# Between two steps of a graph kernel: other work put first, y pairs into period 0, and a list filled in long rows

## The chip, the cores and the metric

The kernel runs on one core of a Trainium2 chip. The metric is the device time of one execution in microseconds (us); the kernel before takes 1303.6 us, the median of three runs (1302.28 to 1304.17).

## The reference

N = 2708 nodes with D = 256 features and a sparse N x N matrix adj (about 0.3% of it, and the diagonal, is not zero). Everything is float32. Cut to what matters:

```python
x  = layernorm(x + relu(concat([x, adj @ x]) @ W0 + b0))          # layer 0
R  = adj + eye(N);  R = R / R.sum(-1)                             # layer 1
Xf = Xa = x;  Z = 0
for n in range(2):
    q, k  = Xa @ W1.T @ W2.T, Xa @ W3.T
    probs = softmax(q @ k.T)
    A     = probs, cut in each row to the largest that hold 0.9 of the mass, made to sum to 1
    Xf, Xa = R @ Xf, A @ Xa
    Z = Z + Xf @ U1[n].T + Xa @ U2[n].T
out = layernorm(x + layernorm(x + Z) * ln_g + ln_b)
```

So there are two attention steps (step 1 and step 2, n = 0 and 1), each with a threshold per row, and two products with R, which don't depend on the attention.

## The kernel before

**Tiling.** The rows are cut into NB = 22 blocks of 128 (the last, EDGE, has 20). Layer 0 runs over the blocks with dense products of adj and y0 = x @ W0's second half (L257; y0 itself is made at the start, L392, from xT, which SP's queue loads in seven pieces at L196). While it does, the columns of adj that are not empty are named, and lists of at most 128 x CC columns (CC = 7) are made for each block: list_d in DRAM is first filled with a default (L280 to L282: a constant in ix, sent out in pieces of seven numbers), and later the names are written over it, and ix is read back from it. With the lists, GpSimd (POOL) gathers rows by indirect DMA: of adj in step 1 (L367, kept in adjc_d), and of the vectors that R is multiplied with (L719).

**Step 1** goes block by block: logits (L507), exp, threshold on VectorE, then turn() transposes the kept probabilities (L527, copied by ScalarE at L530) and products() multiplies them (L564). step1_out returns three pieces of work, scale, turn_out and project (L687 to L703): they scale the result, transpose it into xaT_all, and make from it the query and key of step 2 and a part of Z. The pieces of block t run inside block t + 1; those of the last block, after its edge_sum (L236 to L245), run by themselves. ya_pair (L664 to L678) makes ya, the right side of step 2's products, for two blocks at a time: eight matmuls into one of two acc buffers in PSUM, and a copy by ScalarE. In the kernel before all eleven pairs are put between the steps: one inside edge_sum, one ahead of each piece of the last block, one after each of the logits of blocks 0 to 2, the others after that.

**Step 2** is a software pipeline of NB + 2 periods, each with NG = 6 slots (the loop at L1272 and in it over g). In period per, block per + 2 gets its logits and exps2, block per + 1 its tries of a level (try_act: four passes of ScalarE over a whole row, two in L966 and two in L969, whose output goes to a scratch tile scr that nobody reads), block per its level and candidates and block per - 1 its threshold, marks and mask on VectorE (vector_slots), and block per - 2 its transposes and products. Each engine takes its instructions in the order of this program. Block 0 doesn't get its tries from ScalarE but from VectorE (try_dve) and one pass of ScalarE (L966), all before period 0. The blocks' rows lie in a ring of five tiles: es[2], es[3], es[0], es[1] and a fifth, e4, which with scr shares the place of xaT_all (tag V).

**R's products** are cut into 2 x 22 x 8 = 352 units of two matmuls each (r_units, L749): seven pieces of gathered rows and one of the block's own. The table units says how many each period takes, spread over its slots; first = 16 are taken before period 0. The first unit of a block calls r_load for the next block: its seven gathers on POOL (y_load, two buffers yg, so that a buffer must have been read before), and its loads on SP. r_out scales a finished block on VectorE and SP stores it.

**The end of a block.** When a block has both its parts, a Final does the two layer norms, one period each. final_slot(i) sets their slots: in slot 3 the statistics of both new ones and those in their second norm (finals), in slot 5 the roots on ScalarE, in slot 0 of the next period the normalising on ScalarE and two tensor operations on POOL for each new one (L1207, L1208), which the second statistics (L1182) need.

Of the kernel before, what the change touches and what calls it, by code (L numbers as in the profile page):

```python
# [9 lines left out]
FP = mybir.dt.float32  # L10
I32 = mybir.dt.int32
# [9 lines left out]
P = 128  # L21
# [18 lines left out]
ML = 16  # L40
CW, CC = 128, 7
# [107 lines left out]
def fast_path(ctx, tc, c, flags, fint, xT_d, x_d, w0_d, b0_d, w1_d, w2_d, w3_d, u1_d, u2_d, g_d, b_d):  # L149
    nc = tc.nc  # L150
    N, D, DA, NB, DC, KH, CHS, rows = c.N, c.D, c.DA, c.NB, c.DC, c.KH, c.CHS, c.rows
    ident = c.ident
    adj_d, out_d, x1_d, za_d = c.adj_d, c.out_d, c.x1_d, c.za_d
    NW = SEG * NS
# [14 lines left out]
    def ps_acc(t=None):  # L169
        acc = ps.tile([P, CH], FP, tag="acc", name="acc")  # L170
        if t == NB - 1:
            nc.vector.memset(acc[:, :D + 1], 0.0)
        return acc

    def ps_misc():
        return ps.tile([P, CH], FP, tag="misc", name="misc")
# [56 lines left out]
    fold = small.tile([P, EW], FP, tag="fold", name="fold", bufs=1)  # L233
    nc.vector.tensor_reduce(fold, ident.rearrange("p (j i) -> p i j", i=EW), AX.X, ALU.add)

    def edge_sum(acc, n, stop=True, meanwhile=None):  # L236

        p = rows(EDGE)
        four = work.tile([P, 4, P], FP, tag="wT", name="four", bufs=3).rearrange("p k i -> p (k i)")
        nc.scalar.copy(four[:, :n], acc[:, :n])  # L240
        if meanwhile:
            meanwhile()
        whole = ps_misc() if meanwhile else ps_acc()
        nc.tensor.matmul(whole[:p, :n], lhsT=fold[:, :p], rhs=four[:, :n], start=True, stop=stop)
        return whole  # L245

# [18 lines left out]
    LAST = NB * P * NB - 1  # L265
# [11 lines left out]
    for y_d in (c.yf_d, c.v_d):  # L277
        nc.gpsimd.dma_start(out=y_d[rows(NB - 1):, NB - 1, :], in_=zero)
    ix = small.tile([P, NB, CC], I32, tag="ix", name="ix", bufs=1)
    nc.gpsimd.iota(ix.rearrange("p m c -> p (m c)"), pattern=[[0, NB * CC]], base=LAST, channel_multiplier=0)  # L280
    for i, (a, b) in enumerate(((0, ML), (ML, NB))):
        nc.gpsimd.dma_start(out=c.list_ds[i][:, :CW * CC].rearrange("m (p c) -> p m c", c=CC), in_=ix[:, a:b, :])  # L282
    before_m = small.tile([NB, 1], FP, tag="before_m", name="before_m", bufs=1)
    nc.gpsimd.iota(before_m, pattern=[[0, 1]], base=0, channel_multiplier=KS * CAP,
                   allow_small_or_imprecise_dtypes=True)
# [376 lines left out]
    def ya_pair():  # L662


        if not y_pairs:
            return
        t0 = y_pairs.pop(0)
        pz = ps_acc().rearrange("p (s d) -> p s d", d=D)
        for s in range(2):
            p, at = rows(t0 + s), (t0 + s) * P  # L670
            for j in range(DC):
                nc.tensor.matmul(pz[:p, s, :], lhsT=xaT_all[:, j, at:at + p], rhs=c.u2[:, j, 1, :],  # L672
                                 start=j == 0, stop=j == DC - 1)
        if rows(t0 + 1) == P:
            nc.scalar.copy(ya[:, t0:t0 + 2, :], pz)
            return
        for s in range(2):
            nc.scalar.copy(ya[:rows(t0 + s), t0 + s, :], pz[:rows(t0 + s), s, :])  # L678
# [218 lines left out]
    for t in range(NB):  # L897
        acc = ps_acc(t)
        part = exps1(t + 2) if t + 2 < NB else None
        b = None  # L900
        if t >= NB - 3:
            b = blocks[t - (NB - 3)] = Block(t - (NB - 3))
        ra_next = finish1(t + 1) if t + 1 < NB else None
        for g in range(NG):
            turn(t, g, x1, acc, es[t % 4])
            if ends and 1 <= g <= 3:
                ends[g - 1]()
            if g < NL and t + 3 < NB:
                logits1(t + 3, g)
            if b and g in (0, 2):  # L910
                lg = logits(1, b.t, g // 2)
                if g == 0:
                    shift(b, lg[0])
            if b and g in (1, 3):
                exps2(b, g // 2, *lg)
            if part and g in (3, 4):
                part(g - 3)
            products(1)
            if stores and stores[0][0] <= NG * t + g:
                adj_store(*stores.pop(0)[1:])  # L920
            if g == 2:
                if t + 3 < NB:
                    extract1(t + 3)
                if t < 9:
                    lists.take(2 * t + 2, 2 * t + 4)
                if t == 8:
                    lists.end()
            if (t, g) in at:
                adj_gather(at[t, g])
                stores += [(NG * t + g + i, at[t, g], i - 4) for i in (4, 5)]  # L930
            if (t, g) in y_at:
                name_y()
                y_load(0, y_at[t, g])
            if (t, g) == (NB - 1, 2):
                a_load(0)
        if t == EDGE:
            products(0)
            acc = edge_sum(acc, D, meanwhile=ya_pair)
        ends = step1_out(t, acc, ra)
        ra = ra_next  # L940
    assert not stores and not staged and not to_turn
    r_load(0, 0)
    for f in ends:
        ya_pair()
        f()
    ya_pair()
    for t in range(3):
        exps2(blocks[t], 2, *logits(1, t, 2))
        ya_pair()
    while y_pairs:  # L950
        ya_pair()

    tile1 = big.tile([P, 2 * NW], FP, tag="x1", name="w")
    low = tile1[:, :NW]
    w = tile1[:, NW:]
    tile2 = big.tile([P, 2 * NW], FP, tag="V", name="e4")
    nc.gpsimd.memset(tile2[:, N:NW], 0.0)
    ring.append(tile2[:, :NW])
    scr = tile2[:, NW:]

    def try_act(b, k, part):

# [261 lines left out]
    def final_slot(i):  # L1224


        if i == 2:
            while ready and len(new) < 2:
                new.append(Final(*ready.pop(0)))
                new[-1].load()  # L1230
        if i == 1:
            while done:
                done.pop().store()
        n = len(new) + len(finals)
        if i == 3:
            for k, f in enumerate(new + finals):
                f.stats(k)
        if i == 5 and n:
            roots(0, n)
        if i == 0 and n:  # L1240
            over(0, n)
            for f in finals:
                f.end()
            for f in new:
                f.middle()
            done[:] = finals
            finals[:] = new
            new.clear()
# [3 lines left out]

    each = NB * (CC + 1)
    first = 2 * (CC + 1)
    units = {0: CC + 1, 1: CC + 1}
    rest = each - first - sum(units.values())
    units.update({p: rest * (p - 1) // 8 - rest * (p - 2) // 8 for p in range(2, 10)})
    units.update({p: each * (p - 10) // 11 - each * (p - 11) // 11 for p in range(11, 22)})
    assert first + sum(units.values()) == 2 * each


    b0, b1, b2 = (blocks[t] for t in range(3))
# [7 lines left out]
    try_act(b0, 1, 0)  # L1270
    next_level(b0, 1)
    for per in range(NB + 2):  # L1272
        if per == NB + 1:
            tail.append(True)
        n_r = units.get(per, 0)
        b_act = blocks.get(per + 1)
        t_mul = per - 2 if per > 1 else None
        if t_mul is not None:
            accs[t_mul] = ps_acc(t_mul)
        b_exp = None  # L1280
        if per and per + 2 < NB:
            b_exp = blocks[per + 2] = Block(per + 2)
        vector = vector_slots(blocks.get(per), blocks.get(per - 1), begin_search(b_exp) if b_exp else None)
        for g in range(NG):
            n = n_r * (g + 1) // NG - n_r * g // NG
            now = later.pop(0)
            later.append([])
            if g == 0:
                if b_exp:
                    shift(b_exp, lg[0])  # L1290
                r_units(n)
            if t_mul == EDGE:
                if g == 0:
                    products(0)
                    products(0)
                    edge_product(ya, accs[EDGE], e2(EDGE))
            elif t_mul is not None:
                turn(t_mul, g, ya, accs[t_mul], e2(t_mul))
            if b_exp and g == 3:
                lg = logits(1, b_exp.t, 2)  # L1300
            if g == NG - 1 and 3 < per + 3 < NB:
                lg = logits(1, per + 3, 0)
            if g:
                r_units(n)
            if b_exp and g == 1:
                lg = logits(1, b_exp.t, 1)
            if t_mul is not None and t_mul != EDGE:
                products(2)
            if b_exp and g in (0, 1, 3):
                exps2(b_exp, (g + 1) // 2, *lg)  # L1310
            if b_act:
                for k, part in {0: ((0, 0),), 1: ((0, 1), (0, 2), (0, 3)), 2: ((1, 0),), 3: ((1, 1), (1, 2), (1, 3))}.get(g, ()):
                    try_act(b_act, k, part)
            next(vector)
            if g == 0:
                final_slot(0)
                if t_mul:
                    t = t_mul - 1
                    base = za_load(t)
                    later[1].append(lambda t=t, base=base: arrive(t, base, accs.pop(t), ras.pop(t)[:rows(t)]))  # L1320
            for f in now:
                f()
            if g and (per < NB + 1 or g < NG - 1):
                final_slot(g)
# [407 lines left out]
```

## Time and profile before

| | |
|---|---|
| median of 3 runs | 1303.6 us |
| the profiled execution | 1308.28 us |
| its span, first to last instruction | 1306.5 us |
| TensorE busy | 1236.7 us (95%) |
| VectorE busy | 997.3 us (76%) |
| ScalarE busy | 735.6 us (56%) |
| POOL busy | 641.9 us (49%) |
| mean granted TensorE clock | 0.980 |

In the profile PE is TensorE (PEld its weight loads), DVE is VectorE, ACT is ScalarE, POOL is GpSimd and SP the engine that issues most DMAs; "SPq" and the like are the issue of a DMA. A line of a timeline gives the start, the duration, engine, line of the code, operation and tiles, and in square brackets the idle time ahead of it and what ended it. "x8" at the end of a line says that eight instructions are merged in it. Times of the profile count from the span's start. Layer 0 lasts to about 288 us, step 1 to about 730, step 2 from there to the end.

### The profile page before, as it was taken

Reading aid. Unit: us, or ns where it says so; the run is one execution under the profiler, and the core shown is the slowest. Engines: PE = TensorE matmul, PEld = TensorE weight load, DVE = VectorE, ACT = ScalarE, POOL = GpSimd, SP = SyncE. Lnnn points to the kernel's source line nnn. Section 1 sums busy time; section 2 is a strip of 40 time slices with the busy share of each in tenths; the row PEclk is TensorE's granted clock in tenths of the full one; section 3 lists DMA queues with packets and bytes.
Section 4 is the critical chain, followed back from the end, with each engine's and each line's share of the span. In section 5 each row is a group of like instructions: output and inputs, shape, how many; then the busy total and the mean of one; then the engine's idle time right before and its main releaser. Section 6 shows DMA issues by size and latency. Waiting matters only on the chain.

```text
span 1306.5 us, 18895 instructions
## 1 busy us (share of the span) xinstructions
PE 1236.7 (95%) x5764; PEld 892.9 (68%) x5764; DVE 997.3 (76%) x3406; ACT 735.6 (56%) x1337; POOL 641.9 (49%) x594
## 2 busy tenths in 40 slices
PE   7999999979899999999999978999999999999975
PEld 5878778843477777777777556777765777766753
DVE  2455445884999997977771279989888999999996
ACT  1010110125456656655665488887888989989821
POOL 1000000002465442577666068878775778888850
PEclk9999999999999999999999888999999999999898
DMA  7455445423322220132324145565663645555551
GB/s 189 152 171 165 149 160 169 148 89 105 119 81 84 70 71 12 40 93 92 91 85 107 49 150 156 177 184 169 185 145 114 197 143 161 175 169 156 151 121 38
DMA packets 101704, 166.00 MB, mean 127 GB/s; under 512 B 17362, under 2 KB 74070, under 8 KB 101594
## 3 DMA queue, kind: packets, MB, share of 16 engines
q1 hardware_dynamic: 75308, 108.65, 26.0%
q0 software_dynamic: 20544, 51.17, 15.1%
q10 hardware_dynamic: 5742, 4.89, 1.4%
q8 instruction: 48, 0.79, 0.3%
q14 instruction: 62, 0.51, 0.1%
HBM read 130.74 MB, written 33.90 MB: 126 GB/s over the span
## 4 chain that ended last, share of the span: by engine, by line
PE 77%; DVE 10%; ACT 6%; DMA 3%; POOL 2%; issue 1%; SPq 0%; ACTq 0%; POOLq 0%; DVEq 0%
PE acc L564 26%; PE acc L257 16%; PE lg L507 9%; PE misc L749 9%; PE tr L527 7%; PE acc L651 2%; DVE e L1088 2%; DVE w L1083 2%; PE acc L462 2%; PE misc L426 2%; PE acc L672 2%; PE misc L699 2%; DMA xT<-in_xT 1%; POOL yg L719 1%; ACT e L844 1%
## 5 line engine op out<-in xcount | busy, mean ns | idle before, releaser
L530 ACT COPY wT<-tr 128x512 f32<-128x512 f32 (+2 forms) x258 | 132.0, 519 | 216.8 <-PE tr L527 215.8
L564 PE MATMUL acc<-x,wT 128*128 128x256 f32 (+1 forms) x924 | 230.5, 388 | 0.0
L564 PE MATMUL acc<-ya,wT 128*128 128x256 f32 (+1 forms) x924 | 228.1, 386 | 0.0
L719 POOL DMA_INDIRECT yg<-v_d,ix x154 | 196.6, 1277 | 59.8 <-issue 23.2
L719 POOL DMA_INDIRECT yg<-yf_d,ix x154 | 191.6, 1244 | 48.3 <-issue 23.1
L564 PEld LDWEIGHTS acc<-x,wT 128*128 128x128 f32 (+1 forms) x924 | 165.2, 189 | 71.0 <-issue 37.4
L257 PE MATMUL acc<-y,adj_t 128*128 128x257 f32 (+1 forms) x924 | 208.4, 381 | 0.0
L564 PEld LDWEIGHTS acc<-ya,wT 128*128 128x128 f32 (+1 forms) x924 | 170.6, 191 | 44.5 <-issue 24.0
L749 PE MATMUL misc<-yg,adj_t 128*128 128x256 f32 (+1 forms) x704 | 185.1, 396 | 14.0 <-DMA yg<-v_d,ix 6.6
L257 PEld LDWEIGHTS acc<-y,adj_t 128*128 128x128 f32 (+1 forms) x924 | 171.8, 189 | 32.7 <-issue 8.9
L367 POOL DMA_INDIRECT adj_t<-in_adj,ix x154 | 167.8, 1089 | 51.8 <-issue 44.1
L749 PEld LDWEIGHTS misc<-yg,adj_t 128*128 128x128 f32 (+1 forms) x704 | 124.2, 191 | 67.2 <-issue 21.5
L507 PE MATMUL lg<-k,q 64*128 64x512 f32 (+3 forms) x528 | 150.2, 596 | 14.0 <-ACT e L848 7.0
L527 PE MATMUL tr<-ident,e 128*128 128x128 f32 (+2 forms) x946 | 148.5, 276 | 7.5 <-DVE e L1088 6.3
L527 PEld LDWEIGHTS tr<-ident,e 128*128 128x128 f32 (+2 forms) x946 | 113.0, 140 | 52.1 <-issue 24.0
L334 POOL DMA_DIRECT2D part_d<-e x1 | 0.6, 573 | 290.3 <-DVE e L333 290.3
L966 ACT ACTIVATE e<-e,st 128x2708 f32<-128x2708 f32 (+1 forms) x43 | 113.5, 2640 | 0.1
L439 ACT COPY x1T<-tr 128x256 f32<-128x256 f32 (+1 forms) x22 | 8.0, 364 | 186.6 <-PE tr L438 186.6
L969 ACT ACTIVATE e<-e,st 128x2708 f32<-128x2708 f32 (+1 forms) x42 | 110.9, 2641 | 0.1
L570 DVE MAX8 cand<-e 128x8 f32<-128x170 f32 (+1 forms) x352 | 87.2, 317 | 26.6 <-ACT e L514 26.6
L1030 DVE MAX8 cand<-w 128x8 f32<-128x136 f32 (+1 forms) x440 | 105.9, 284 | 0.0
L1083 DVE MATCH_REPLACE8 w<-part,e 128x680 f32<-128x680 f32 (+1 forms) x88 | 74.3, 850 | 0.0
(238 smaller groups left out, 1732.3 us busy)
## 6 DMA issues: line engine op xcount, KB each, us to landing
adj_t<-in_adj SPq DMA_DIRECT2D x44, 704.0 KB
adj_t<-adjc_d SPq DMA_DIRECT2D x44, 448.0 KB
adjc_d<-adj_t SPq DMA_DIRECT2D x22, 256.0 KB
base<-za_d SPq DMA_DIRECT2D x40, 128.0 KB
adjc_d<-adj_t SPq DMA_DIRECT2D x22, 192.0 KB
xt<-in_x ACTq DMA_DIRECT2D x21, 128.0 KB
x_d<-x SPq DMA_DIRECT2D x21, 128.0 KB
x1b_d<-xb SPq DMA_DIRECT2D x21, 128.0 KB
```

Source lines behind the costliest of these rows:

```text
L257: nc.tensor.matmul(acc[:p, :n], lhsT=halves[k // KH][:kw, k % KH, :p], rhs=y[:kw, k, :n], start=k == 0, stop=stop and k == NB - 1)
L367: nc.gpsimd.indirect_dma_start(out=a[:CW, i, :], out_offset=None, in_=adj_rows, in_offset=bass.IndirectOffsetOnAxis(ap=ix[:CW, m, i:i + 1] ...
L507: nc.tensor.matmul(lg[:p, h, :b - a], lhsT=q[o, t * P:t * P + p], rhs=keys[s][o, i, :b - a], start=True, stop=True)
L527: nc.tensor.transpose(tr[:kw, k % 4, :p], e[:p, k * P:k * P + kw], ident[:p, :p])
L530: nc.scalar.copy(wT[:, :full, :p], tr[:, :full, :p])
L564: nc.tensor.matmul(acc[:p, :D], lhsT=wT[:kw, k % 4, :p], rhs=y[:kw, k, :], start=k == 0, stop=k == NB - 1)
L719: nc.gpsimd.indirect_dma_start(out=y[:CW, i, :], out_offset=None, in_=rows_d, in_offset=bass.IndirectOffsetOnAxis(ap=ix[:CW, m, i:i + 1], ...
L749: nc.tensor.matmul(acc[:p, :D], lhsT=a[:kw, k, :p], rhs=y[:kw, k, :], start=k == 0, stop=k == CC)
L966: nc.scalar.activation(scr[:b.p, :N], e, AF.Relu, bias=b.nz, scale=b.l[k], accum_out=b.relu)
L969: nc.scalar.activation(scr[:b.p, :N], e, AF.Sign, bias=b.nz, scale=b.l[k], accum_out=b.sign)
L1030: nc.vector.max(b.cand[:p, 8 * i:8 * i + 8], low[:p, SEG2 * i:SEG2 * (i + 1)])
L1083: nc.vector.match_replace(w[:b.p, W * i:W * (i + 1)], b.part[:b.p, i, :], e2(b.t)[:b.p, W * i:W * (i + 1)], 3.0e38)
```

## The change

Five edits:

1. The default of list_d is no longer written into ix and sent in pieces of seven numbers: a constant is written into es[2] (16 partitions, 896 numbers each), and each of the 22 rows of list_d is filled from one partition.
2. Between the steps no y pair is made any more. The chain of the last block (edge_sum, scale, turn_out, project) runs straight through, then the third logits and exps2 of blocks 0 to 2, then, as before, the logits of block 3, R's first 16 units and ScalarE's pass over block 0.
3. scr is at first es[1], which step 1 no longer needs and block 3 takes in period 1. The tile of the fifth row and the later scr is taken at the start of period 1 (fifth), with its memset on POOL.
4. In period 0 each slot makes two y pairs (eleven in all), and slots 3, 4 and 5 take 2, 3 and 3 of R's units. Period 0 and 1 had 8 units each; period 1 now has 16, and periods 2 to 9 share 136 instead of 144.
5. The statistics of finals move from slot 3 to slot 4.

```diff
-    def edge_sum(acc, n, stop=True, meanwhile=None):
+    def edge_sum(acc, n, stop=True):
...
-        if meanwhile:
-            meanwhile()
-        whole = ps_misc() if meanwhile else ps_acc()
+        whole = ps_acc()
...
-    nc.gpsimd.iota(ix.rearrange("p m c -> p (m c)"), pattern=[[0, NB * CC]], base=LAST, channel_multiplier=0)
+    fill = es[2][:max(ML, NB - ML), :CW * CC].bitcast(I32)
+    nc.gpsimd.iota(fill, pattern=[[0, CW * CC]], base=LAST, channel_multiplier=0)
     for i, (a, b) in enumerate(((0, ML), (ML, NB))):
-        nc.gpsimd.dma_start(out=c.list_ds[i][:, :CW * CC].rearrange("m (p c) -> p m c", c=CC), in_=ix[:, a:b, :])
+        nc.gpsimd.dma_start(out=c.list_ds[i][:, :CW * CC], in_=fill[:b - a])
...
-            acc = edge_sum(acc, D, meanwhile=ya_pair)
+            acc = edge_sum(acc, D)
...
     for f in ends:
-        ya_pair()
         f()
-    ya_pair()
     for t in range(3):
         exps2(blocks[t], 2, *logits(1, t, 2))
-        ya_pair()
-    while y_pairs:
-        ya_pair()
...
-    tile2 = big.tile([P, 2 * NW], FP, tag="V", name="e4")
-    nc.gpsimd.memset(tile2[:, N:NW], 0.0)
-    ring.append(tile2[:, :NW])
-    scr = tile2[:, NW:]
+    scr = es[1]
+
+    def fifth():
+        nonlocal scr
+        tile2 = big.tile([P, 2 * NW], FP, tag="V", name="e4")
+        nc.gpsimd.memset(tile2[:, N:NW], 0.0)
+        ring.append(tile2[:, :NW])
+        scr = tile2[:, NW:]
...
         if i == 3:
-            for k, f in enumerate(new + finals):
+            for k, f in enumerate(new):
                 f.stats(k)
+        if i == 4:
+            for k, f in enumerate(finals):
+                f.stats(len(new) + k)
...
-    units = {0: CC + 1, 1: CC + 1}
-    rest = each - first - sum(units.values())
+    units = {0: 0, 1: 2 * (CC + 1)}
+    rest = each - first - (CC + 1) - sum(units.values())
...
     for per in range(NB + 2):
+        if per == 1:
+            fifth()
...
+            if per == 0:
+                ya_pair()
+                ya_pair()
+                r_units((CC + 1) * max(0, g - 2) // 3 - (CC + 1) * max(0, g - 3) // 3)
             next(vector)
```

More of the change, by code (lines that the diff above doesn't have):

```diff
@@ L1254, in fast_path @@
     first = 2 * (CC + 1)
-    units = {0: CC + 1, 1: CC + 1}
-    rest = each - first - sum(units.values())
+    units = {0: 0, 1: 2 * (CC + 1)}
+    rest = each - first - (CC + 1) - sum(units.values())
     units.update({p: rest * (p - 1) // 8 - rest * (p - 2) // 8 for p in range(2, 10)})
     units.update({p: each * (p - 10) // 11 - each * (p - 11) // 11 for p in range(11, 22)})
-    assert first + sum(units.values()) == 2 * each
+    assert first + (CC + 1) + sum(units.values()) == 2 * each
     b0, b1, b2 = (blocks[t] for t in range(3))
```

## The prediction

> **What bounds the kernel now.** I read the page first (busy times, slices), then the chain of waits, then windows cut at the periods of the second attention step, and then each engine's timeline around the places that the diff touches.
>
> ```profile
> PE 1236.7 (95%) x5764; PEld 892.9 (68%) x5764; DVE 997.3 (76%) x3406; ACT 735.6 (56%) x1337; POOL 641.9 (49%) x594
> ```
>
> TensorE is busy 95%, so only places where it waits or is slow can give anything. There are three. The first is the start:
>
> ```profile
> 3.44 16.70 DMA xT<-in_xT
> 21.16 9.85 PE misc L392 x36
> ...
> DMA packets 852, 1.12 MB, mean 372 GB/s; under 512 B 50, under 2 KB 637, under 8 KB 852
> ...
> q0 software_dynamic: 58, 0.07, 18.6%
> ...
> DMA packets 154, 0.27 MB, mean 89 GB/s; under 512 B 15, under 2 KB 31, under 8 KB 154
> ```
>
> The two chain lines say that the load of xT held everything until 20.1 us. The DMA views of 3-6, 9-12 and 12-15 us say why: 372 GB/s falls to 89 GB/s, while the engines stay busy. The fall comes when queue 0 moves 0.07 + 0.01 MB (9 to 15 us). Those are the two fills of list_d (56 + 21 KB) from ix, in pieces of CC*4 = 28 bytes.
>
> The second place is the gap between the steps:
>
> ```profile
> 756.31 2.65 ACT L966 ACTIVATE e<-e,st 128x2708 f32<-128x2708 f32 x1
> 772.83 1.09 ACT L844 ACTIVATE e<-lg,nmax 128x1024 f32<-128x1024 f32 x1
> ...
> 786.56 2.08 PE L507 MATMUL lg<-k,q 64*128 64x512 f32 x4 [5.17 <-ACT e L844]
> 788.57 4.55 PE L749 MATMUL misc<-yg,adj_t 128*128 128x256 f32 x10
> ...
> 755.86 0.11 POOL L957 MEMSET e<- 128x12 f32 x1 [40.22 <-PE acc L672]
> 757.70 0.95 POOL L719 DMA_INDIRECT yg<-yf_d,ix  x1 [1.68 <-PE misc L749]
> ```
>
> ScalarE's pass over block 0 (L966, into scr) starts only when the last y pair has freed xaT_all; from then to 790.4 ScalarE never stops and TensorE waits for it. POOL stood idle for 40 us first.
>
> The third is the stretch that follows, in windows of one period each (length, then busy time of PE, PEld, DVE, ACT, POOL, clock, DMA):
>
> ```profile
> 835.80:859.60 23.80, 23.80 (x115) 18.00 (x115) 20.97 (x77) 19.95 (x34) 19.23 (x16) 1.00 0.57 166
> 1170.60:1195.80 25.20, 23.56 (x110) 16.80 (x110) 23.75 (x87) 22.30 (x39) 20.93 (x19) 1.00 0.54 165
> ...
> DVE bst L1182 <- POOL yg L1208: 6.5, 10, 0.9
> 1262.79 0.43 DVE L1182 BATCH_NORM_STATS2 bst<-yg 128x6 f32<-128x256 f32 x1 [0.84 <-POOL yg L1208]
> ```
>
> At 836 TensorE is full for the whole period. At 1170 it isn't; but POOL is: 20.9 us busy plus 0.30 us ahead of each of 15 gathers is 25.4 of 25.2 us. POOL gathers without a pause from 757.7 to 976.1 and again from 990.5 to 1259.7. VectorE then waits 6.5 us, in ten pieces, for POOL before its statistics.
>
> **What the Trainium skill says.** "DMA: Bandwidth & Descriptors", Specifications: a transfer needs at least 512 B for line rate, below that there is a read-modify-write. The trace agrees (89 against 372 GB/s with 28-byte pieces in flight), though it doesn't show the pieces apart. "TensorE: Matmul & The Clock Gate", Part 1: TensorE's clock halves after an idle window of about 3.4 us, windows run free. The trace agrees: after 5.2 us idle ten matmuls took 4.55 us, where six otherwise take 1.46. A window 58% busy (779 to 783) caused no drop, one 41% busy (718 to 721) did. "SBUF — State Buffer", Who interferes with whom: a VectorE instruction with two SBUF inputs contends with a GpSimd one that reads SBUF. The trace agrees: gathers take 0.95 us, but 3.42 when L1088 runs (1142.8), two such in each period.
>
> **Part by part.** All sums are against the profiled execution: 1308.28 us, of which the span is 1306.5 and 1.8 lie around it. The median of the runs is 1303.6, 0.36% less; I take the same microseconds off it.
>
> 1. Fill from es[2]. Removed: 2816 pieces of 28 bytes. Added: 22 rows of 3584 bytes, and an iota 896 wide in place of 154; at the old 0.29 us per 154 columns it is at most 1.7 us, on POOL, whose next consumer (the ones in y0) is due at 33 us: nothing. What it releases: L392 is 88 matmuls. Eight ran by 8.20, forty took 8.90 us (0.2225 each). If TensorE never waits for xT or a blocked ScalarE DMA issue, the 80 left end at 8.67 + 17.8 = 26.5 instead of 31.0: 4.5 us. Late next is TensorE itself; adj for m = 0 would land by about 15 us (5 MB at 372 GB/s). Bounds: 0 (the fall has another cause) and 5. I take **4.4 us**; all of stage 1 is TensorE's and moves with it.
>
> 2. Last chain first. The products of the last block end at 730.0. Now: copy 0.4, fold 0.54, scale 0.5, transposes and copy 0.5, projections 1.3, with no y pair between; the logits of b0 start at 733.4 instead of 741.5. Each of three logits (1.06) and exps2 (0.9) alternate: b0's sum at 735.4 (before 743.5), the last exps2 at 739.4 (749.4), logits of block 3 to 740.5. R's 16 units (32 matmuls of 0.217) run 740.5 to 747.5 instead of 756.8 on. VectorE's two try_dve end at 744.5 instead of 752.5; then ScalarE's small steps, and its pass over block 0 (L966) lies before that, at 740.3. ScalarE is free for period 0 at 745.0 instead of 759.5. za_d's store and a_load(1) on SP move forward by 6 us and stay ahead of block 1.
>
> 3. Eleven y pairs in period 0. They cost TensorE 1.80 us each (four took 7.21) and ScalarE 0.57 each. Only two acc buffers: a pair waits for the copy two back, and the copies are queued behind that slot's pass (2.77 or 3.93 us). Slot by slot this gives TensorE waits of 1.55, 0.3 and 0.65 us; 747.5 + 19.8 (11 pairs) + 2.2 (the five units ahead of the last pair) + 2.5 (waits) = 772.0, the last copy at **772.5**. Behind the last pair wait the memset of the fifth block on POOL, and the gathers of block 4; and ScalarE's period 1, which began at 772.83 before. So **14 us gained on ScalarE are given back to the y pairs**: 0.3 us net. Period 1 is ScalarE's as before (17.6 us), TensorE idles some 4 us again and drops to half clock again. R's 16 units there fit into the idle time; the gathers of block 4 start at 772, its last piece lands by 787, is due at 789.
>
> 4. Units shared anew. Periods 2 to 9 have 136 instead of 144 units: 8 x 0.433 = 3.5 us off a full TensorE. POOL has 14 gathers done at 772 instead of 12; its last of the first product ends earlier by 2 x 1.25 + some hidden long ones, 3.7 to 5.2 us; so the short stalls for yg (943, 965 us; some 2 us) mostly go. Parts 2 to 4 together: bounds 0 and 8 (no half clock in period 1 would add 3); I take **4.3 us**, between TensorE's 3.8 and POOL's 5.2.
>
> 5. finals' statistics in slot 4. No work removed. VectorE's two marks (2 x 0.85) now lie under POOL's tensor ops. But POOL sets the pace here (25.2 us a period), so the 6.5 us of waits can't all go: VectorE's gain is used up after one period, and only the last one's counts: the mask at 1267.2 comes after two marks less. **1.7 us**; bounds 0 and 6.5.
>
> Sum 4.4 + 4.3 + 1.7 = 10.4: profiled 1297.9, median **1293.2**.
>
> **Rivals.** (B) The fall of the DMA rate has another cause, such as the loads of adj themselves; the start stays. For it: the rate recovers only slowly after 15 us. Against: later loads of adj alone move 158 GB/s with the engines busy half the time. 1303.6 - 6.0 = 1297.6. (C) The thin stretch from 730 to 740, where TensorE is about 55% busy, halves the clock; the y pairs end 3 us later, POOL's gathers with them: parts 2 to 4 give about 0, 1297.5. The windows known lie at 41% (drop) and 58% (none). (D) Period 1 keeps its clock, or more stalls go: 1289. (E) Slower: y pairs and passes fall into step, TensorE waits in every slot for ScalarE and works period 0 at half clock: 19.8 + 3.5 us of work cost 23.3 more, less 10.4: 1316.5. It decides from 10.4 us lost, 21 us at half clock on end; against it, no drop so far lasted over 6.9 us, as TensorE is then full.
>
> **How the numbers follow.** The forecast 0.55; B 0.14; C 0.14; D 0.08; B with C (1302) 0.05; E 0.04. The likeliest is 1293.2. The range 1288.5 to 1299.5 takes in D, B and C; left out are E, B with C, and better than D. The measurement of this kernel can't tell less than about 0.2% (2.6 us) from no change; B with C is "same". Faster 0.91, same 0.05, slower 0.04.
>
> **What would show it.** Right: L392 ends near 26.5 and the DMA rate stays over 300 GB/s to the end of xT; L966 for block 0 near 736 after that shift; ScalarE's period 1 (L844) starts as late as before, less 4.4; the first product's last gather 8 to 9 us earlier; no VectorE wait of note on L1208 but about as long periods after 1145. Wrong: L392 still at 31; half clock between 730 and 770; gathers stalled behind L957.

## The result, and the profile after

Before 1303.57 us median (12 runs, 1300.42 to 1304.71), after 1302.28 (12 runs, 1298.16 to 1306.05): ratio 0.9992 [0.9979, 1.0004]. In a second comparison, on another chip, the changed kernel took 1299.85 against 1302.70, ratio 0.9979 [0.9966, 0.9992]. So the change gives 1.3 us, which the comparison can't tell from nothing, or 2.9 us, and not 10.4.

The two profiled executions stand further apart than that: 1308.28 us before, longer than any timed run of it, and 1298.16 after, the shortest of its 12. The experiments therefore began with the unchanged kernel traced once more. It is called "before, second trace": 1302.78 us, span 1301.0. One of the chips used later ran every kernel 3 to 4% longer, with pauses that the trace doesn't explain; ratios on it are to the kernel before on the same chip, and of its times only the first and the last microseconds of the traces are set beside others. There the changed kernel was the slower one (1.0039).

**TensorE as a whole**, from the pages: first before in its second trace, then after.

```profile
PE 1232.0 (95%) x5764; PEld 890.1 (68%) x5764; DVE 997.7 (77%) x3406; ACT 735.6 (57%) x1337; POOL 638.9 (49%) x594
```

```profile
PE 1229.2 (95%) x5764; PEld 889.5 (69%) x5764; DVE 995.8 (77%) x3406; ACT 734.9 (57%) x1337; POOL 638.1 (49%) x594
```

**The start.** DMA in the window 9 to 12 us and the chain of waits up to 27 us, before in its second trace:

```profile
DMA packets 208, 0.34 MB, mean 113 GB/s; under 512 B 35, under 2 KB 73, under 8 KB 208
```

```profile
0.75 3.89 DMA e<-in_w
...
8.93 17.87 PE misc L392 x80
```

The same two of after:

```profile
DMA packets 737, 1.21 MB, mean 405 GB/s; under 512 B 81, under 2 KB 337, under 8 KB 737
```

```profile
0.75 3.72 DMA e<-in_w
...
8.76 17.69 PE misc L391 x80
```

The rate falls with the short pieces, as the prediction had it, and stays up without them. But in these two traces the 80 matmuls run without a pause: the fall is hidden behind TensorE. In the first trace of before it was not, but TensorE lost far less there than the 16.70 us of the chain:

```profile
18.04 1.10 PE L392 MATMUL misc<-e,xT 128*128 128x256 f32 x4 [0.47 <-DMA xT<-in_xT]
21.16 9.83 PE L392 MATMUL misc<-e,xT 128*128 128x256 f32 x36 [2.02 <-ACT y L395]
```

It waited 2.5 us, and the half clock that followed cost another 1.7: in the last trace below, of the units and the statistics, the same 36 matmuls take 8.14 us. In that trace and in one of the units alone the chain also runs over xT (14.54 and 14.45 us): xT lands at 17.8 us there, at 20.1 in the first trace of before; why so late is not known. Both have y0 done at 27.0 us. In all eleven other traces with the short pieces it is done at 26.4 to 27.2 us, in the eight without them at 26.1 to 27.3.

**The gap**, in the timeline of after:

```profile
729.74 1.12 PE L506 MATMUL lg<-k,q 64*128 64x512 f32 x4 [1.03 <-ACT e L843]
731.87 1.50 PE L506 MATMUL lg<-k,q 64*128 64x512 f32 x4 [1.01 <-ACT e L843]
734.38 2.08 PE L506 MATMUL lg<-k,q 64*128 64x512 f32 x4 [1.01 <-ACT e L843]
736.38 8.60 PE L748 MATMUL misc<-yg,adj_t 128*128 128x256 f32 x32
...
783.31 1.75 PE L506 MATMUL lg<-k,q 64*128 64x512 f32 x4 [2.56 <-ACT e L843]
```

```profile
734.65 2.65 ACT L964 ACTIVATE e<-e,st 128x2708 f32<-128x2708 f32 x1 [0.32 <-DVE bulk L851]
...
769.12 0.11 POOL L955 MEMSET e<- 128x12 f32 x1 [10.95 <-PE acc L671]
769.78 0.95 POOL L718 DMA_INDIRECT yg<-yf_d,ix  x1 [0.55 <-issue]
```

Four logits matmuls need 1.12 us, then 2.08: the clock is at half, and it stays there for the first of R's 32 matmuls behind them (8.60 us; 7.17 at full clock in the second trace of before). ScalarE's pass over block 0 is early, as forecast (734.65), and POOL's memset waits for the last pair as forecast.

**The later periods**, from one block's mask to the next's (length, then busy time of PE, PEld, DVE, ACT, POOL, clock, DMA), before in its second trace and after:

```profile
849.43:873.22 23.79, 23.02 (x111) 16.83 (x110) 21.18 (x77) 19.94 (x34) 19.22 (x16) 1.00 0.59 179
1136.96:1162.14 25.18, 24.63 (x118) 18.12 (x117) 23.74 (x86) 23.46 (x46) 20.90 (x19) 1.00 0.53 165
```

```profile
900.90:924.25 23.35, 23.35 (x114) 17.60 (x113) 20.98 (x78) 19.93 (x34) 18.78 (x16) 1.00 0.58 182
1133.81:1157.57 23.76, 23.22 (x111) 16.85 (x110) 23.52 (x87) 22.15 (x40) 19.78 (x18) 1.00 0.51 162
```

The regular length of periods 2 to 9 is 23.35 us instead of 23.79, about the two matmuls of one unit less (0.217 us each). Of the eight intervals from the mask of block 1 to that of block 9, five are longer than regular before (24.1 to 25.3 us) and one after (24.65). Of the five periods of some 25 us near the end, the lines show the one that gained most; all five together fall from 124.8 to 122.6 us. VectorE's wait for POOL before its statistics is as long as it was, in fewer pieces. From the waits of after:

```profile
DVE bst L1180 <- POOL yg L1206: 6.5, 6, 1.8
```

### The profile page after: what moved, and what is told of

Read it like the earlier page. It is cut to its first block, busy times and chain, and to the rows that moved or that the text cites. A ratio compares the mean times of both kernels' runs of the same rounds, so it can differ in the third digit from the quotient of the medians.

```text
span 1296.4 us, 18890 instructions
## 1 busy us (share of the span) xinstructions
PE 1229.2 (95%) x5764; PEld 889.5 (69%) x5764; DVE 995.8 (77%) x3406; ACT 734.9 (57%) x1337; POOL 638.1 (49%) x594
## 3 DMA queue, kind: packets, MB, share of 16 engines
q0 software_dynamic: 20528, 51.17, 14.4%
## 4 chain that ended last, share of the span: by engine, by line
PE 76%; DVE 8%; ACT 6%; DMA 4%; POOL 3%; issue 3%; POOLq 0%; ACTq 0%; DVEq 0%
PE acc L563 25%; PE acc L255 16%; PE lg L506 9%; PE misc L748 8%; PE tr L526 7%; DMA yg<-v_d,ix 3%; PE acc L650 2%; POOL yg L718 2%; PE acc L461 2%; PE misc L391 2%; PE misc L425 2%; PE misc L698 1%; DVE e L1086 1%; DMA yg<-yf_d,ix 1%; ACT e L843 1%
## 5 line engine op out<-in xcount | busy, mean ns | idle before, releaser
L748 PE MATMUL misc<-yg,adj_t 128*128 128x256 f32 (+1 forms) x704 | 184.3, 394 | 13.7 <-DMA yg<-v_d,ix 10.1
L366 POOL DMA_INDIRECT adj_t<-in_adj,ix x154 | 164.8, 1070 | 51.3 <-issue 41.0
L506 PE MATMUL lg<-k,q 64*128 64x512 f32 (+3 forms) x528 | 150.4, 597 | 13.7 <-ACT e L843 6.7
```

The source lines that it names most:

```text
L366: nc.gpsimd.indirect_dma_start(out=a[:CW, i, :], out_offset=None, in_=adj_rows, in_offset=bass.IndirectOffsetOnAxis(ap=ix[:CW, m, i:i + 1] ...
L506: nc.tensor.matmul(lg[:p, h, :b - a], lhsT=q[o, t * P:t * P + p], rhs=keys[s][o, i, :b - a], start=True, stop=True)
L748: nc.tensor.matmul(acc[:p, :D], lhsT=a[:kw, k, :p], rhs=y[:kw, k, :], start=k == 0, stop=k == CC)
```

## The experiments

Theory after the result: the start gives nothing; the thin stretch behind the last block halves TensorE's clock (the prediction's rival C) and delays period 2; the fewer units win that back; the statistics gain. Rival: the parts gain what was forecast and hinder each other when together. All runs of a group stand beside the kernel before on the same chip.

**First four: the kernel before again, and each part alone.**

> The kernel before once more, for a second trace of it. If its first trace is a fair picture: y0 (L392) ends near 31.0 us, period 1 of ScalarE starts near 772.8, the last mask near 1282.6, span near 1306. If the first trace was a slow execution, as its 1308.28 us against a median of 1303.6 suggest, the span is 1300 to 1303 and the 4 us are missing in one stretch; whichever stretch that is also says what the change had less to gain from.

Measured: 1302.32 us, ratio 1.0006 [0.9994, 1.0017]. Its trace is the one shown above.

```diff
-    nc.gpsimd.iota(ix.rearrange("p m c -> p (m c)"), pattern=[[0, NB * CC]], base=LAST, channel_multiplier=0)
+    fill = es[2][:max(ML, NB - ML), :CW * CC].bitcast(I32)
+    nc.gpsimd.iota(fill, pattern=[[0, CW * CC]], base=LAST, channel_multiplier=0)
...
+        nc.gpsimd.dma_start(out=c.list_ds[i][:, :CW * CC], in_=fill[:b - a])
```

> Only the fill of list_d from es[2] is changed. Theory: the short pieces slow the DMA at the start in every execution, TensorE is 4.5 us ahead from 26.5 us on and all later stages move with it: about 1299, ratio 0.9966. Rival 1: the fall of the DMA rate happened in the profiled execution alone: ratio 1.000. Rival 2: the 4.5 us are had at the start and lost again by the gap between the steps, which is held by something that doesn't move (ratio 0.999 to 1.000, but L392 ends at 26.5).

Measured: 1302.97 us, 1.0003 [0.9994, 1.0013]. In its trace the rate from 9 to 12 us is 405 GB/s, as in after. Hence the old fill causes the fall, and in the median the fall costs nothing. (The new fill also reads from 16 partitions instead of 128; that it is the length of the pieces that counts was not tried apart.)

```diff
         if i == 3:
-            for k, f in enumerate(new + finals):
+            for k, f in enumerate(new):
                 f.stats(k)
+        if i == 4:
+            for k, f in enumerate(finals):
+                f.stats(len(new) + k)
```

> Only the statistics of finals are moved to slot 4. Forecast: 1.7 us faster (ratio 0.9987), VectorE's waits on POOL (L1208) shorter in the periods after 1145 us but those periods still about 25 us long, since POOL's gathers set them. Rival: VectorE set them: 6 us faster (0.995). Rival: nothing (1.000), the mask of the last period waits for POOL as before.

Measured: 1298.85 us, 0.9974 [0.9965, 0.9982].

The order between the steps and the units together (edits 2 to 4 of the change, nothing else):

> All of the gap between the steps, fifth and the units, without the new fill and with the statistics in slot 3. Forecast: 4.3 us faster (0.9967). Rival (C of the prediction): TensorE's thin work behind the last block halves its clock, the y pairs end later and with them ScalarE's period 1 and the gathers of block 4: 0 to 4 us slower (1.000 to 1.003), with weights of 0.217 us per matmul doubled in R's first 16 units and period 2 starting later, counted from the end of the last block's products, than in the kernel before.

Measured: 1303.06 us, 1.0003 [0.9992, 1.0013]. So the statistics are the only part that gains by itself.

**Second four, on the chip that runs everything longer** (the kernel before 1352.62 us there).

> The changed kernel once more, beside the kernel before on the same chip. Theory (the order between the steps costs 3.3 us at the start of period 2, fewer units regain about that by period 9, and the statistics give 3.9): the parts add up, 1299 us, ratio 0.997. Rival (the order between the steps takes back some 2.7 us when the statistics are moved too, as the first comparison of 0.9992 suggests): 1301.7, ratio 0.999.

> The change without its order between the steps: only the fill and the statistics. Theory: the fill gives nothing and the statistics 3.9 us, ratio 0.997, about 1299 us. Under the rival of the run before, it is 2.7 us faster than the whole change on the same chip; under the theory, they are equal within a microsecond.

> The kernel before with only R's units shared out as in the change: 16 instead of 8 in period 1, and 136 instead of 144 in periods 2 to 9; y pairs, last chain and scr as before. Theory (what the change wins back in periods 2 to 9 is the eight units fewer, 3.5 us of a full TensorE, and period 1 has room for them, since TensorE idles there some 4 us): 2 to 3.5 us faster than before, ratio 0.9975 to 0.998, and period 2 starts as late as before. Rival (period 1's room is used up by TensorE's half clock, or the gathers of block 4 come too late for period 1): period 2 starts 2 to 4 us later and the ratio is 1.000.

> The kernel before with R's units shared out as in the change and the statistics of finals in slot 4, nothing else. Theory: both gains add up, 1302.9 - 3 - 3.9 = 1296 us, ratio 0.995, better than both kernels. Rival (the two are one gain: POOL sets the pace from period 15 on, and what is saved in periods 2 to 9 is waited for there): 1299 us, ratio 0.997.

Measured, in this order: 1.0039 [1.0021, 1.0057], 0.9981 [0.9960, 1.0002], 1.0003 [0.9983, 1.0023], 0.9996 [0.9976, 1.0016]. The chain of waits of the units alone has a pause in period 1, just where the units had been put:

```profile
794.31 2.63 ACT e L966 x2
796.94 15.92 another core or an unknown queue
812.85 0.02 issue
```

On this chip the whole change is slower than before. What period 1 or the units are worth can't be read from such traces; the questions were put again.

**Third four, on another chip.**

> The changed kernel again, since the chip of the last four runs ran every kernel some 50 us longer, with pauses of several us in which no engine waited for anything that the trace shows. If the chip runs the kernel before in about 1303 us: the parts add up (0 + 0 - 3.9), 1299 us, ratio 0.997; or the order between the steps takes part of it back, 1301.5, ratio 0.999. In the trace: period 2 starts some 64.8 us after the last block's products, and TensorE is at half clock from 8 to 15 us after them.

Measured: 1299.85 us, 0.9979 [0.9966, 0.9992].

> The fill and the statistics without the order between the steps, beside the whole change on one chip. Theory that the parts add up: equal to the whole change within 1 us. Rival: 2.5 to 3 us faster than the whole change.

Measured: 1300.15 us, 0.9981 [0.9970, 0.9993], as much as the whole change: the order and the units are worth nothing also when the statistics are in.

```diff
     for f in ends:
         f()
+        r_units(n)
     for t in range(3):
-        exps2(blocks[t], 2, *logits(1, t, 2))
+        lg = logits(1, t, 2)
+        r_units(4)
+        exps2(blocks[t], 2, *lg)
...
-    r_units(first)
```

(n is 2, 1, 1 for the three pieces.)

> The whole change, but R's first 16 units no longer follow the logits of block 3 in one piece: two after the last block's scale, one each after its turn and its projection, four each between the logits and the exps2 of blocks 0 to 2, so that TensorE has no thin stretch. Theory (the thin stretch halves the clock and that costs 2.5 to 3.3 us): no half clock between 8 and 15 us after the last products, period 2 starts 61.5 us after them instead of 64.8, and the time is 2.5 to 3.3 us less than the whole change: 1296. Rival (ScalarE and the copies of the y pairs hold period 2, not the clock): half clock gone, but period 2 starts as late as in the whole change and the time is the same.

Measured: 1297.88 us, 0.9953 [0.9935, 0.9971], in six runs. Its timeline in the stretch that was thin:

```profile
733.70 1.99 PE L748 MATMUL misc<-yg,adj_t 128*128 128x256 f32 x8
735.62 1.12 PE L506 MATMUL lg<-k,q 64*128 64x512 f32 x4
736.67 1.99 PE L748 MATMUL misc<-yg,adj_t 128*128 128x256 f32 x8
738.60 1.12 PE L506 MATMUL lg<-k,q 64*128 64x512 f32 x4
739.65 1.99 PE L748 MATMUL misc<-yg,adj_t 128*128 128x256 f32 x8
741.57 1.13 PE L506 MATMUL lg<-k,q 64*128 64x512 f32 x4
```

Every group of four logits matmuls takes 1.12 us, with nothing but the order of the same instructions changed. The new order does two more things: it fills the idle times between the groups, and it starts R's gathers 2.0 us after the last block's products instead of 14.0. Period 2 starts 61.4 us after the last block's products; in the whole change it was 64.8 and 65.2.

```diff
-    units = {0: 0, 1: 2 * (CC + 1)}
+    units = {0: 0, 1: CC + 1}
```

(on the order and units of the fourth run: the order alone is left)

> The kernel before with the order between the steps alone: last chain straight, all y pairs in period 0, scr in es[1] at first; R's units as many as before in periods 1 to 9 (8 in period 1, 144 in periods 2 to 9; the 8 of period 0 stay there, in its slots 3 to 5), fill and statistics as before. Theory (the order costs 3.3 us at period 2 and the eight units fewer win it back): 3 us slower than before, ratio 1.0025, period 2 later by 0 to 3.3 us. Rival (the earlier gathers win it back, not the units): within 1 us of before.

Measured: 1307.48 us, 1.0027 [1.0015, 1.0039]. Period 2 starts 64.6 us after the last products.

**Fourth four, again on the longer chip** (the kernel before 1346.47 us).

> The kernel before with only R's units shared out as in the change (16 in period 1, 136 in periods 2 to 9), y pairs and last chain as before. Theory (the units are what wins back the cost of the order): periods 2 to 9 at 23.35 us instead of 23.8, ratio 0.9975 to 0.9985, less than the 3.5 us of eight units, since POOL starts the gathers of period 1 late. Rival (period 1 has no room): period 2 starts 3 us later and the ratio is 1.000.

> The kernel before with the units shared out as in the change and the statistics of finals in slot 4. Theory that the gains add up: ratio 0.995 to 0.996, 1297 us, as good as the whole change with a full TensorE. Rival: 0.998, as the statistics alone.

> The order between the steps and the units, with R's first 16 units put between the pieces of the last chain and the logits of blocks 0 to 2 (TensorE full there); fill and statistics as before. Theory (half clock in the thin stretch is the whole cost of the order): 2.5 to 3.5 us less than the order and units without it, ratio 0.9975, 1299.5 us. Rival (the gain of the earlier run came from few runs): ratio 1.000.

> The whole change with R's first 16 units put between the pieces of the last chain and the logits, once more. Theory: 0.995 to 0.996, 1297 us, the lowest of the four. Rival: 0.998, as the whole change itself.

Measured, in this order: 1.0009 [0.9992, 1.0026], 0.9986 [0.9958, 1.0013], 0.9974 [0.9956, 0.9991], 0.9953 [0.9932, 0.9974]. The full TensorE has the same ratio on both chips, and with the fill and the statistics left out it still gains.

**Last two, on the first chip** (the kernel before 1303.91 us).

```diff
-    units = {0: CC + 1, 1: CC + 1}
+    units = {0: CC + 1, 1: 2 * (CC + 1)}
```

> The kernel before with R's units shared out as in the change, once more. Theory: periods 2 to 9 take 23.35 us each, so that the time from the mask of block 1 to that of block 8 is 163.5 us instead of the 166.5 to 167 that eight units more give; period 2 starts 0 to 2 us later than before after the last products; ratio 0.998 to 0.9985. Rival (period 1 has no room, the gathers hold its units): period 2 starts 3 us later and the ratio is 1.000.

> The kernel before with the units shared out as in the change and the statistics in slot 4, once more. Theory: 0.9955, 1297 us. Rival: as the statistics alone, 0.9975.

Measured: 1305.09 us, 1.0007 [0.9998, 1.0017], and 1302.05 us, 0.9984 [0.9971, 0.9996]. The theory was wrong here, its rival right: period 2 starts 67.0 us after the last products. In the old order POOL begins R's gathers 27.7 us after these products, with the new order 14.4, and TensorE waits for the gathers in period 1 and is at half clock there for 13.7 us. The units alone:

```profile
779.03 1.13 PE L749 MATMUL misc<-yg,adj_t 128*128 128x256 f32 x4 [2.21 <-DMA yg<-yf_d,ix]
780.09 1.97 PE L507 MATMUL lg<-k,q 64*128 64x512 f32 x4
781.99 3.78 PE L749 MATMUL misc<-yg,adj_t 128*128 128x256 f32 x8
787.80 1.22 PE L749 MATMUL misc<-yg,adj_t 128*128 128x256 f32 x2 [2.03 <-DMA yg<-yf_d,ix]
788.95 2.08 PE L507 MATMUL lg<-k,q 64*128 64x512 f32 x4
```

So the units need the order: with it, eight units more in period 1 put period 2 off by 0.2 us (64.6 to 64.8), without it by 5.5 (61.5 to 67.0).

## Why the prediction was wrong

The account below cuts one trace of each kernel at five points: the end of the last block's products in step 1; the first transpose of period 2; the start of the last block's mask (L1088); the end of the last instruction, which is VectorE's (L1190); the end of the span. It leaves out all that lies before the first point, where a half-clock stretch at about 717 to 728 us comes in some executions of either kernel and costs about 3 us.

| us | to period 2 | to the last mask | to the last instruction | to the end | sum |
|---|---|---|---|---|---|
| before, second trace | 61.5 | 491.4 | 18.0 | 5.8 | 576.7 |
| statistics alone | 61.5 | 488.8 | 16.3 | 6.0 | 572.5 |
| order alone | 64.6 | 487.1 | 17.9 | 8.0 | 577.7 |
| units alone | 67.0 | 484.8 | 18.0 | 6.0 | 575.7 |
| order and units | 64.8 | 484.1 | 18.0 | 8.2 | 575.1 |
| after | 64.8 | 483.2 | 16.3 | 8.2 | 572.5 |
| full TensorE | 61.4 | 482.6 | 18.0 | 8.2 | 570.2 |

**Step 1, 4.4 us: failed.** The step read the fall of the rate rightly (113 to 405 GB/s) and failed in the term after it, "what it releases": it took the waits of one execution, with 16.70 us of chain for xT, for a property of the kernel. Even there the load of xT did not hold everything until 20.1 us: TensorE lost 4.2 us, 2.5 by waiting and 1.7 by the half clock behind. In the second trace the short pieces are there, the fall is there, and L392 ends at 26.8 us, about where the prediction had put it for the changed kernel; in every trace but the first it ends at 26.1 to 27.3. Rival B named the outcome, but not the reason: the fall has the cause that was forecast, and it is hidden. That removes 4.4 of the 10.4 us.

**Steps 2 to 4, 4.3 us: failed in two terms, and a third came out larger.** The forecast was that period 2 starts no later. It starts 3.3 us later (64.8 against 61.5): the step counted the logits at 1.06 us and R's 32 matmuls at 0.217 us each, and the thin stretch halved the clock under them. R's first units end 21.1 us after the last products instead of 17.5; the half clock is 2.8 of these 3.6 us, by the durations shown above (1.50 and 2.08 instead of 1.12, 8.60 instead of 7.17). This is rival C, which was given 0.14, with its mechanism and its 3 us; the prediction dismissed it because a window 58% busy had caused no drop (the trace has 2.18 us of 4.00, 55%, from 779 to 783), and it counted the stretch as 55% busy on the whole. But the stretch is uneven. The windows of after, 3.4 us each, cut backwards from the drop at 732.5, and ahead of them one that was not followed by a drop:

```profile
715.40:718.80 3.40, 1.66 (x13) 0.48 (x13) 0.00 (x0) 2.05 (x7) 0.00 (x0) 1.00 0.00 0
722.30:725.70 3.40, 2.38 (x18) 0.70 (x16) 0.00 (x0) 1.07 (x4) 0.00 (x0) 1.00 0.17 49
725.70:729.10 3.40, 2.72 (x14) 1.14 (x12) 0.41 (x1) 1.01 (x5) 0.00 (x0) 1.00 0.03 6
729.10:732.50 3.40, 1.75 (x8) 0.60 (x8) 2.57 (x7) 1.49 (x4) 0.00 (x0) 1.00 0.75 227
```

70%, 80%, then 51%, and the drop. In the trace of the order alone the window ahead of its drop (at 731.3) holds 1.75 us as well, in order and units 1.36 (40%). The busy share alone doesn't decide, since the window at 715.4, 49% busy, was not followed by a drop; which work counts for how much was not tried. With the full TensorE the half clock in this stretch and the 3.3 us are gone, but that run doesn't part the clock from the idle time: the y pairs start 15.6 us after the last products instead of 21.0, and of these 5.4 us, 3.3 are idle time that R's units now fill and 2.1 shorter work; 3.4 us are left at period 2. That the clock cost the forecast some 3 us rests on the durations above. The Trainium skill, "TensorE: Matmul & The Clock Gate", Part 1, A second HAM failure mode: psum-queue depth-cycling, says of another kernel that frequent short idle times between groups of matmuls make the clock swing as well; this trace agrees in so far as the clock fell with idle times of only 1.01 to 1.03 us.

The term that came out larger is what follows, from period 2 to the last mask: 7.3 us less in the order and units (491.4 to 484.1), where 3.5 us of units and some hidden stalls were counted. TensorE from the start of period 2 to the mask of block 9, in before's second trace, in the order alone, and in order and units:

```profile
785.78:997.40 211.62, 203.86 (x966) 147.67 (x965) 186.66 (x682) 176.42 (x288) 158.54 (x128) 1.00 0.58 169
```

```profile
787.24:994.56 207.32, 202.13 (x966) 148.29 (x965) 184.94 (x672) 176.17 (x288) 154.92 (x125) 1.00 0.59 170
```

```profile
791.83:996.18 204.35, 199.36 (x952) 145.72 (x951) 184.43 (x669) 176.12 (x288) 150.60 (x125) 1.00 0.58 168
```

The first step, 4.3 us, is the order's: idle time of TensorE falls from 7.8 to 5.2 us as the gathers come earlier (its waits for yg from 3.3 to 1.2), and it is 1.7 us less busy. The second, 3.0 us, is the units'.

The other failed term stands nowhere in the prediction: between the last instruction and the end of the span lie 5.8 to 6.0 us in all twelve traces with the old order, and 8.0 to 8.3 us in all eight with the new one. The DMA queues of that stretch, in the statistics alone and in after:

```profile
q14 instruction: 6, 0.05, 2.0%
```

```profile
q14 instruction: 7, 0.06, 1.8%
```

One more packet of instructions is moved, in each of the eight. That it makes these 2.0 to 2.5 us was not tried. So in the traces of order and units and of before 3.3 and 2.4 us are lost and 7.3 won: 1.6 less, and nothing in the medians.

**Step 5, 1.7 us: right in kind, too small.** The statistics alone give 4.1 us in the medians (1302.92 to 1298.85; 2.3 to 4.6 by the interval of the ratio) and 2.5 with the fill on another chip. The step's own term, the last mask, came 2.6 us earlier instead of 1.7, 2.2 of it in the five long periods, where the gain was not used up after one. POOL's last gather ends where it did (1254.3 and 1254.1), as it should if POOL sets the pace. The rest is a term that was not counted, the last block's products. Before's second trace, then the statistics alone:

```profile
1282.48 4.99 PE L550 MATMUL acc<-ya,wT 128*20 128x256 f32 x44 [0.60 <-ACT wT L546]
```

```profile
1280.22 3.30 PE L550 MATMUL acc<-ya,wT 128*20 128x256 f32 x44 [0.60 <-ACT wT L546]
```

At full clock they take 1.7 us less. Of the 20 traces, eleven had the statistics in slot 4, and in eight of these they took 3.3 us (4.8 to 5.0 in the other three, the full TensorE among them); in eight of the nine others, 4.9 to 5.0. That VectorE would have "no wait of note" was wrong (6.5 us still).

**The slower rivals and the range.** TensorE and ScalarE did not fall into step: in after the clock is full from 739.3 to 783.7, so E is out. Of D, the stalls that go came true. The case "B with C", 1302, is nearest to what happened, and it was given 0.05. That its number is met (1302.28) is partly luck: it has steps 2 to 4 at nothing and step 5 at 1.7 us, while the runs have losses and a larger gain in the former and a larger gain in the latter. The other error lies ahead of all steps: the sum was made against an execution 4.7 us longer than the median, and 4.2 us of that were its own start, which step 1 then sold as a gain.

**Still open.** The order alone is 3.5 us slower by its ratio (4.8 by the medians), but 1.0 in its trace. Its 22 runs fall into two groups, eight with a span of 1300.3 to 1302.9 and a mean clock of 0.980 or 0.981, 14 with 1305.0 to 1307.9 and 0.974 to 0.979; the profile is of the first. An estimate from these figures: 0.006 of clock are about 16 us more at half clock (0.006 x 1300 / 0.5), worth up to 8 us; where they lie was not traced. The same holds for the first 12 runs of after: ten lie below 0.980.

## What to carry to other kernels

A stall seen in one profiled execution is a candidate, not a fact: trace the unchanged kernel a second time before a gain is counted on it, above all where that execution is longer than the timed runs. When a change makes a stretch tidy (chain first, bulk work after), look whether it leaves TensorE half busy for a few microseconds: it then stands idle, and its clock may fall. The same bulk work placed between the steps of the chain cost nothing here, and gave the lowest ratio of all, 0.9953 on two chips. And a place for more work has to be checked for its inputs as well as for its engine: the free time in period 1 was TensorE's, but the gathers were not there.

## What the runs showed of the hardware

- TensorE's clock fell to half after windows of 3.4 us that were 51% busy (after, order alone) and 40% busy (order and units), with no single idle time over 1.03 us. The busy share alone doesn't decide: in after a window 49% busy (715.4 to 718.8) was not followed by a drop, and in before's second trace the clock fell at 1282.6 after one 76% busy, which held 22 transposes of 20 x 20 (L544).
- The drops of a trace lie on a grid: in after the first four begin at 275.1, 288.8, 340.0 and 732.5 us, 4, 15 and 115 times 3.413 us apart.
- Two transfers of 77 KB in all, in pieces of 28 bytes, hold all DMA traffic of the core at 89 to 125 GB/s (9 to 15 us, both traces of before), where 405 and 411 are moved without them; in all twelve traces with the old fill it is 75 to 135, in the eight with the new one 398 to 421. The Trainium skill, "DMA: Bandwidth & Descriptors", Specifications, states a price (a read-modify-write below 512 B) for the short transfer itself; the runs show one for what moves beside it.
- The end of the program, from the last instruction on, took 8.0 to 8.3 us in every trace of the new order and 5.8 to 6.0 in every one of the old, with one more packet of instructions.
- The same program took 1302.7 to 1303.9 us on two chips and 1346.5 to 1352.6 on a third, whose traces have pauses of up to 15.9 us.
